# A new order of steps and of PSUM places in a one-core kernel of shift-mix, state space, attention and two mixture-of-experts stages

## The chip, the cores and the metric

The kernel runs on one core of a Trainium2 chip. The metric is the device time of one execution in microseconds. The engines are named as the profile names them: PE (TensorE, matrix products), PEld (its weight loads), ACT (ScalarE), DVE (VectorE), POOL (GpSimd) and SP (SyncE, which only issues transfers).

## What is computed

The input x has 1024 tokens of width 256, all in float32. Each stage adds its result to x. In shortened form:

```
x += shift_mix(norm(x))             # keys, values, receptance, a scan over time, an output product
x += first_ffn(norm(x))             # 8 experts, the best one of each token
x += state_space(norm(x))           # projection, convolution, scan in blocks, gated norm, output product
x += first_ffn(norm(x))             # the same weights again
x += attention_a(norm(x))           # 16 heads of 16 in 4 groups, causal
x += second_ffn(norm(x))            # 32 experts, the best 4 of each token, silu(gate) * up, down
x += attention_b(norm(x))           # 16 heads, 4 shared keys and values, a slope for distance
x += second_ffn(norm(x))            # the same weights again
```

An expert stage has to take to each expert the tokens that chose it, and to bring its rows back, weighted.

## The kernel before

**Groups and streams.** The tokens are cut into two groups of 512 (four tiles of 128). Each stage of each group is written as Python generators ("streams"); one call of a stream emits one step, a few instructions. A stream's name is a letter for the stage, the group, and a letter for the kind of step. The stages are A (shift-mix), F (first experts), S (state space), G (first experts again), a (attention a), e (second experts), b (attention b) and f (second experts again). So F1s is the sending of group 1's tokens to the first experts, and e0d the down products of group 0 in the second experts. Names without a group (k1, kf, la, lf, ls, l1, lw, cl, x0, x1, PS, P2) are loads, constants, clears and the switch between memory pools.

**The order is written out.** A string `ORDER` (L39 on) lists 2431 steps, and `follow` (L119) takes one step of the named stream for each entry. Every engine works its own instructions in the order in which they were emitted, and waits by semaphore for what it needs of others. A second string, `BANKS` (L105 on), gives each PSUM tile in turn one of eight places (`bank`, L142); a tile waits until the one before it in its place has been read.

**The expert stages.** In the second experts (`second_ffn`, L984) the steps are r (route: norm, logits, the four best, and ranks counted by matmuls at L1013 to L1018), s (16 sends by index on POOL, L1046, one for each tile and choice, which scatter rows of xn to a buffer in HBM sorted by expert), w (weights), f (16 fetches of a pair of experts by SP, L1073), t (turn: px transposes at L1082 on PE, copied to xT by ACT at L1086), g (gate: pgu products at L198, silu on ACT at L1098, a product on DVE at L1100), h (turn back: ph transposes at L1107, copied to hT by DVE at L1110), d (down: py products at L1118, copied to ye by DVE at L1122, stored by SP at L1124), b (16 fetches by index on POOL, L1134) and a (16 adds to x on DVE, L1144). xe has three buffers, xT, he, hT and ye two, yb six. The first experts (`first_ffn`, L374) do the same with eight experts: ranks at L415 to L419, four sends by index at L448, four fetches at L476, px at L483, xT at L488, py by L198, four fetches by index at L512, adds at L521.

```
for t in range(NT):
    for j in range(TOPK):
        nc.gpsimd.indirect_dma_start(
            out=sent_to[g][t * TOPK + j],
            out_offset=bass.IndirectOffsetOnAxis(ap=to[:, t, j:j + 1], axis=0),
            in_=xn[:, t, :], in_offset=None, bounds_check=ROWS - 1,
            oob_is_err=False)
        yield
```

**What lies beside what.** One group's experts are emitted between the steps of the other group's work. POOL has, beside the sends and fetches by index, the causal selects of the attention stages (L904), some row additions, small powers (L193) and a few constants. At the end the 16 fetches of f1b and their adds have nothing left beside them.

Of the kernel before, what the change touches and what calls it, by code (L numbers as in the profile page):

```python
# [36 lines left out]


ORDER = """  # L39
k1 A0n kf x0*2 kf A1n A0n*2 x0 A0n x0 A0n*3 la A0n*4 lf x1 A1n x1 A0n ka A0m0 x1 A1n*2 A0n*2 A0m0  # L40
x1 A1n*2 A0m0 la lf A0m0 A0k0 A0m2*2 A1n*3 A0m1 A1n A0m1*3 A1n*2 A1m0 A0k0*4 A0k1*5 A0k0*2 ls A0k0
la A0v0 A1m0 la lf*2 A1n lf A1n A1m0*2 A0m2 A0b A0v0*2 A0k1 kf A0v0*2 A0k1 A0m2 ls A0k1 A0m2 ls*2
A1k0*3 A0v1 A0r0*2 A0v1*2 A1k0 A0v1 lf A0v1 A0r1*2 A1m1 A1k1 la A0o A1k1*4 A0o*4 F0r*2 A0o*3 F0r*2
A1m1*2 F0r A1m1 A1v1 lf*2 F0r A1k1*2 A1m2 F0r*3 A1v0 A1v1*3 F0r*3 A1k1 A1v1 k1*2 ks kf*3 F0r*5 ls
k1 A1k0*2 A1m2*4 F0r*3 F0s*4 A1v0*2 F0f A1v0 A1k0*2 A1v0 A1r0*2 A1r1*2 A1b A1o*3 F1r A1o ks*3
A1o*3 F1r*2 F0f F0t A1o F1r*2 PS F0t*2 F0f*2 F0t*2 F1r*4 F0e F1r*3 lf F0e*2 F0t F0e*2 F1r*5 F0e*2
F0r F0t F1r*4 F1s F0e*2 F1s F0t F0e*3 F1s*2 F0w F0b F0a S0n F0b*2 F1f F0a F0b F0a S0n*2 F0a S0n
F1f S0n F1t*3 F1w F1e F1t F1f*2 F1t ks*2 S0n*8 F1e*3 F1t*3 S0d*2 F1e*3 S0d*5 S0u*2 S0c*3 S0h S0u
S0c*2 F1e*2 S0h*2 S0g*2 S0h F1e*2 S0h*5 S0c*5 F1e S0h*4 F1b S0g*5 F1a S1n F1b*3 S0g k1 F1a S0c*2
F1a S1n*2 F1a S1n*2 cl*2 S0h*4 S0d*2 S1n*3 k1 S0l*2 S1n S0m*4 k1 S0l*3 S0h*3 k1 S0h cl S0h*2 S1n*4  # L50
S0l cl S0l*3 S1g*2 S1c S1d*2 S1c*4 S0u*2 S0h S0v*2 S0l*2 S0v S1d S0v*3 S0l S0v S0l S1d S0u*2 S1d
S0o S0u S1h S0v*5 S0y S1h S0o*2 S0y*2 S0l*2 S0y S0z S0o S1c S1h S1g S0z*2 S1h S0z S1d S1h S1c
S1h*4 S0l S0z S1c S0o*3 S1h S0z*4 S1c*2 S0z S1h S0z*3 S0y S0z*4 l1*2 G0r S1d S0l*4 S1u*2 S0l S1c
S1h*6 S1c S0z*2 S0l G0r S0l S1u*2 S1h*3 cl S0l S0y*2 S1h*3 S0y S0z*2 S1h l1 S0z S0o S0z S1g*2 S1d
cl S1v S1d S1v*7 S1m*4 S1l*2 S0z*5 S1l*2 cl S0z*4 S1v*2 S0z*2 S1u*2 S0z*2 G0r S1v*2 S1l*3 S0z*2
G0r*2 S1l*5 S1o S1y*2 G0r S1u G0r S1u G0r*2 S1y*2 S1z G0r*4 k1 S1o*3 S1z*3 G0r S1g*3 G0r*4 S1z
G0r*2 G0w G0s*4 S1z G0f S1z*3 S1l G0f S1z*2 S1l*10 S1z*5 S1l S1z S1y*3 S1z*2 S1o*3 G0t S1y G0f
G0t*2 G0f l1 S1z*2 G0e*3 G0t*2 S1z G0t G0e*2 G0t*2 G0e S1o S1z*2 G0e*2 G1r*2 S1z G0e*4 S1z*10 l1
S1z*3 G0b G1r G0b G1r*2 G0b*2 G1r*6 G0a k1*3 G1r*3 G0a a0n*2 G0a a0n G0a a0n*9 G1r*3 a0n a0k a0q
G1r P2 a0q cl a0a cl*2 a0q*5 G1r*2 G1w a0k*5 a0p k1 G0r k1 a0p k1 G1s a0p cl*2 a0q a0p*7 a0v l1*2  # L60
a0b G1r a0b cl*3 a0p*2 a0v a0p G1s*3 G1f G1t*2 G1f G1t*2 a0p*3 G1f G1t G1f a0p*3 G1e*6 G1t*2 a0b
G1e*2 a0p G1e G1t G1e*2 a0p*4 a0w*6 a0b a0p*5 a0w*4 a0c a0p G1e G1b*3 G1a*2 a1n a0w G1b a0w*6
a0b*2 a0c a0f*3 G1a a1n*2 a0w*3 cl G1a lw*3 a0w*9 a0c a1n a0w a1n*2 a0w*3 a0p a0w*4 a0f a1n*4
a0p*2 a0f a1a a0p a0f*2 a1n*3 a0f e0r a0p*2 a0c a1k a0w*4 a0b a0f a0b a1k a0f a1q*4 a0w*4 a0c
a0w*4 a1q a1k a0f a1k*3 a0w*3 a1p*2 a0f*2 a1q a0f e0r a0f*3 l1*2 a1q*2 a0f*2 a1p*4 a0c a0f*5 a1p*2
a0f*3 a1p a0f e0r*3 a1b*2 a1p e0r*4 a1w*5 a1p*3 e0r a1p*2 e0r*9 a1w a1v*2 a1w*2 a1p*2 a1w e0r*3
a1w a1c a1f a1p*2 a1b*2 e0s a1p*5 e0s*4 a1p a1w*7 a1p*4 e0s*2 a1p*3 a1w*2 a1c lw*2 e0s*3 a1w*3 e0s
a1p*2 a1w*4 lw*4 a1b*2 a1w*3 a1f*2 a1w a1f*2 a1p*2 a1c a1w*3 a1c a1f lw e0s*3 e0w a1f*2 e0s*2 a1b
lw*2 e1r lw a1f*2 a1w*5 a1f a1b a1w*10 a1c a1f*5 e0f*2 e0t e0f*2 a1w*2 a1f a1w e0t a1w a1c a1f e0t
a1f*5 e0t a1f e0g a1f*2 e0g*4 a1f e0t*4 e0h e0g a1f e1r*4 e0h*3 e0g*4 e0f*2 e0t e1r*4 e0g e0d*2  # L70
e1r*4 e0d*2 e1r e0h e0d*2 e0g e0t e1r*2 e0g e0h*3 e0t*2 e1r*2 e0g e1r e0f*3 e0d*2 e0g*4 e0t*2 e0f
e0t e0d*2 e0t*2 e1r*2 e1s*5 e0h*3 e0g*4 e0t*2 e0f e0d*4 e1s e0g*2 e0f e0g e0t*3 e0f e1s e0f e0h*4
e0d*2 e0g e0d e1s*2 e0g*4 e0d*3 e0t*2 e0h e0g e0t*3 e0h*3 e0d*2 e0f*2 e0h e0g*3 e0d*3 e0g e1s*2
e0g e0d*5 e0h e0g e0h*2 e0t*4 e0g*2 e0d*2 e0g e0d e0h*3 e0d*2 e1s*4 e0d e1s e1f*2 e0g*4 e0h*2 e0d
e0g e0d e0t e0g*2 e1f e0h e0d*2 e0g e0h e0d e0h*2 e0d*3 e1t*3 e1f e0d*2 e1t e1g*2 e0d*2 e0b e1t*2
e1g*2 e1t e1h e1g*3 e1f e1h*2 e1f e1g e1h e1d*2 e1f e0b*2 e1d*2 e1g e1t e1g*3 e1t*2 e0b e1t*3
e1h*3 e1d e1g e1h e1f*3 e0a*4 b0n e1g*4 e1t e1d*2 e1t*2 e1d*3 e0b*2 e0a e1d*2 e0a e1h*2 e0b e0a
e1g*5 e1t*3 e1h e1g e1h e1f*3 e1g e0b*3 e1t e1d*5 e1h e1w e1h e0a b0n e1h e1g*3 e1t*2 e1d*2 e1h
e1g e1d e0b e1h e0b*2 e1t e1g e1d e1f e0a e1d e0b e1g*2 e0a*2 e1f e1t*2 e0b*2 e1d*2 e1h e1d e0a*5
e1t e1g*3 b0n*2 e1h*4 e1g*3 b0n e1g*2 b0n*4 e1d*2 e1t*2 e1d*2 b0a e1h*3 e1g e1t b0n*3 e1d*4 e1g*2  # L80
e1t e1d b0n b0q*2 e1g*3 e1d e1h*2 b0k*3 e1d*3 b0q*2 e1h b0k*2 b0q b0k b0p*2 b0q*3 e1f e1t b0p*3
e1t e1g*2 b0p e1g e1d e1h e1d e1h e1d b0b*2 e1h*2 b0p*3 b0w*4 e1d*5 b0p b0w*2 e1d b0p*4 b0w b0p*2
b0w b0p*2 b0w*2 b0v*2 b0b*2 e1d e1b e1a e1b*3 b0p*2 b0w b0p*4 e1a*2 e1b*2 b0w*2 b0c b0p*2 e1a e1b
e1a b0f*3 e1b e1a e1b b0p*4 e1b b0w*6 e1a b0c b0w*3 b0f b0p*3 b0w*4 e1a b0f*3 b0c b0f b0b*2 b0p*2
b0f*2 e1a*2 b0w*6 b0f*2 b0w*2 e1b*3 b1n b0c e1b*3 b0p b0b b0w*3 b0b e1a*3 b0w e1a b0w*6 e1a b0w*4
b0c e1a b0w*4 b1n*4 b0f*5 b1n*2 b0c b0f*3 b1n*3 b0f*4 b1n*3 b1k f0r b1k*3 b0f b1k b0f b1q*2 b0f
f0r b0f b1k b1q e1r b1q*2 b1p f0r*7 b1q*3 f0r*2 b1p f0r*2 b1p*2 f0r b1p*2 b1b f0r*2 b1b b1w*2
f0r*3 b1p*2 b1w*2 b1a b1p b1w*2 f0r*2 b1v*2 b1p*4 b1w b1p b1w*3 b1c b1p*4 b1f*2 b1p b1f b1b*2
b1p*3 f0s b1f b1p*3 b1f f0s*5 b1w*7 f0s*4 b1c b1w*7 b1p*5 b1f b1p*2 b1b*2 b1f b1w*2 b1c b1f b1p*2
f0s*4 b1p*2 b1w*7 b1b b1f f1r b1c f0s*2 f0f b1w*6 f0f b1w b1f b1b b1w b1f b1w*2 b1c b1w*2 b1f*6  # L90
b1w*3 f1r f0t b1w*4 b1f*2 b1c f0t b1f*4 f0g b1f*2 f0t f0f b1f*3 f1r*3 f0t f0g*5 f0f*2 f0t*4 f0h*3
f0g f0t f0g f1r f0f f1r*7 f0f*2 f0d f0g f1r f0h f0d*3 f0t*2 f1r*2 f0h f0d f0g*2 f0h f1r f0g f1r*2
f0g*3 f0t*3 f0d*3 f0h f0g f0t*2 f1r*2 f1s f0h*3 f0g*6 f0f f0t f0d*2 f0h f0d f1w f1s f0h f0f*3
f1s*2 f0d*2 f0h*2 f0d f0t*4 f0g f1s*4 f0g*4 f0d*2 f0f f0d*3 f0t*2 f0d f1s f0h*4 f0g f0f*2 f0g f0t
f0g*3 f1s f0g f0h f1s f0d*3 f0g f0d f0h f0t*2 f0d*2 f0f f1s*2 f0g*2 f0d*2 f0t f0d f0h f0d f0h*3
f0g*3 f0d*2 f0t*4 f0d*2 f0g*2 f1s*3 f1f*2 f0h*2 f0d*2 f0g*2 f0r f1f f0d f0g f0h*2 f0t f0g f0d f0g
f0d f0h*2 f0d f0g f1t*2 f0g f0h f1t*2 f1f*2 f0d*3 f1g*5 f1h f1t*2 f0d*2 f1t*2 f0h f0d f1g*2 f1h
f0d f1g*3 f1t f1h f1f*2 f0d f1d f1g f1t*3 f1f f1g*2 f1h*2 f1t f1d f1f f1g*3 f1d*2 f0w f1t f1h*4
f0b f1f f1t*3 f1d*3 f1g*3 f1h f1f f1t f1d*2 f1g f0b f1d f0a f1h*2 f1t f1d*2 f0a f1d f1g*2 f1d*3
f0b*3 f0a f1h f1f*2 f0a f0b f0a f1h f0b*2 f1g*5 f0b*2 f1d*5 f1h f1t f1g*3 f1t*4 f1h f0a f1h*2 f0b  # L100
f1h f0a f1f f1d*3 f0a f1g*2 f1t*2 f1d f1g*3 f1h f1f f0a*2 f0b f1d*3 z0*2 f1g*2 f1d*2 f1h*2 f1g*2
f1t*2 f1h*2 f1f f0b*3 f1d*6 f1t*2 f1g*3 f1h*2 f1g*2 f1h*2 f1d f1t f1r f1t f1g f1d f0a f1d*3 f1h
f1d f1h f1g f0b f1g*2 f1d f1h*2 f1d*5 f1b f0a*5 f1a f1b f1a f1b*3 f1a f1b*2 f1a*4 f1b f1a f1b*2
f1a f1b f1a*2 f1b f1a z0*2 z1*3 f1b*3 f1a*3 f1b f1a z1
"""  # L105


BANKS = """
012345670132465710324657132405713240537214063752140376215047632041763542076315247063201475147024
730247516204651247051624751602345160234602534602153460215346250734625073153416207543207413674213  # L110
056743025617432561743257641570321574032157430625741302657431027460253174602135674506724150367250
472502347165037146035274160532746105327465320714632140573106735406315047350647135076340753164075
364107534067134075163075146053714635071634056314075604751046351704635170463517043651074365107465
310740574603714603571430571430671430675140367514036275103462751034627103426710213416347106327016
203472013467210462731046237104237610427310642710346207416074601247602471620714607124627150246175
041627504162750412605174621504165720146570124657102465710432
"""

def follow(streams, order):  # L119
# [1509 lines left out]
```

## Time and profile before

| | us |
|---|---|
| runs | 785.84, 787.01, 790.27, 793.4, 797.79 |
| their median | 790.27 |
| the profiled execution | 786.36 |
| its span in the profile | 784.6 |
| DVE, ACT, POOL idle in the span | 295.4, 526.1, 498.0 |
| first and last matmul | 7.30, 752.3 |
| one send by index on POOL, and from one to the next | 0.98, 1.28 |
| one fetch by index, and from one to the next | 1.00, 1.31 |

The times in the profile are counted from the start of its span. In its rows an instruction stands with start, length, engine, line, operation, what it writes and reads, how many are taken together, and in brackets how long the engine had been idle before it and what ended that ("issue" and "remote" mean that the profile shows no such end, or one from outside the engine's own records). PEclk is the clock that PE was granted, as a share of the full one; in the page's row of slices it stands in tenths.

### The profile page before, as it was taken

The page shows a single profiled execution, that of the slowest core. Times are in us where ns is not written, and L with a number is a line of the kernel's source. Part 1 is how long each engine was busy: PE and PEld are TensorE (multiplying, and loading weights), DVE is VectorE, ACT ScalarE, POOL GpSimd, SP SyncE. Part 2 cuts the span into 40 slices and gives each one's busy share as a digit, 9 for nine tenths or more (in the row PEclk, how much of TensorE's full clock was granted, in tenths as well). Part 3 has the DMA queues.
Part 4 walks back from the last instruction along what each step waited for, and adds up shares of the span by engine and source line. Part 5 has one row for each costly group of instructions (what it writes and reads, how often), then busy time and mean ns, then how long its engine had stood idle before and what let it go on. Part 6 is the DMA issues. An engine that isn't in the chain of part 4 may idle for free. (4 is left out here: it accounts for less than half of the span.)

```text
span 784.6 us, 10048 instructions
## 1 busy us (share of the span) xinstructions
PE 642.4 (82%) x3168; PEld 432.7 (55%) x3168; DVE 489.2 (62%) x1507; ACT 258.5 (33%) x476; POOL 286.6 (37%) x333
## 2 busy tenths in 40 slices
PE   5657599999896999987994979999978999599930
PEld 2235464557584554443693968653443369498820
DVE  7987456998646676685371447577786537144642
ACT  4431134775521234322540222323520454122200
POOL 3124322443526234137216053136435421604435
PEclk9997889999896999998997998999997899899975
DMA  6602428000047238802245566212001124456833
GB/s 199 232 0 93 162 69 277 1 1 1 20 143 264 81 102 254 251 24 85 79 135 189 158 206 187 81 62 70 18 2 67 45 91 148 161 175 208 248 104 102
DMA packets 70827, 94.01 MB, mean 120 GB/s; under 512 B 6896, under 2 KB 60656, under 8 KB 70128
## 3 DMA queue, kind: packets, MB, share of 16 engines
q1 hardware_dynamic: 62944, 72.31, 28.7%
q0 software_dynamic: 7680, 20.98, 8.4%
q8 instruction: 27, 0.44, 0.3%
q14 instruction: 32, 0.26, 0.1%
q10 hardware_dynamic: 144, 0.01, 0.0%
HBM read 50.29 MB, written 42.99 MB: 119 GB/s over the span
## 5 line engine op out<-in xcount | busy, mean ns | idle before, releaser
L1134 POOL DMA_INDIRECT yb_f<-done,bk_f x64 | 65.2, 1019 | 110.8 <-issue 38.5
L198 PE MATMUL pgu_f<-gu,xT_f 128*128 128x192 f32 x512 | 98.0, 340 | 2.6 <-ACT xT_f L1086 2.5
L198 PEld LDWEIGHTS pgu_f<-gu,xT_f 128*128 128x128 f32 x512 | 88.9, 200 | 5.8 <-ACT xT_f L1086 3.9
L1046 POOL DMA_INDIRECT sent<-xn_f,to_f x64 | 62.9, 982 | 60.5 <-issue 19.4
L1118 PE MATMUL py_f<-dw,hT_f 96*128 96x256 f32 x256 | 67.5, 391 | 6.0 <-DVE hT_f L1110 5.4
L864 DVE CUSTOM_DVE_ANT_0 junk_b<-pS_b,tri 128x128 f32<-128x128 f32 (+1 forms) x128 | 45.7, 357 | 23.3 <-PE pS_b L851 15.5
L1122 DVE COPY ye_f<-py_f 128x512 f32<-128x512 f32 x64 | 43.8, 687 | 25.0 <-PE py_f L1118 9.1
L1098 ACT ACTIVATE he_f<-pgu_f 128x192 f32<-128x192 f32 x64 | 21.2, 332 | 106.5 <-PE pgu_f L198 55.9
L864 DVE CUSTOM_DVE_ANT_0 junk_a<-pS_a,tri 128x128 f32<-128x128 f32 (+1 forms) x128 | 45.7, 357 | 16.4 <-PE pS_a L851 6.6
L1118 PEld LDWEIGHTS py_f<-dw,hT_f 96*128 96x128 f32 x256 | 45.9, 195 | 13.2 <-ACT he_f L1098 4.4
L1100 DVE TENSOR_TENSOR he_f<-he_f,pgu_f 128x192 f32<-128x192 f32 x64 | 22.0, 349 | 47.9 <-ACT he_f L1098 29.5
L1086 ACT COPY xT_f<-px_f 128x512 f32<-128x512 f32 x64 | 36.6, 588 | 44.4 <-PE px_f L1082 25.0
L1110 DVE COPY hT_f<-ph_f 96x256 f32<-96x256 f32 x64 | 26.1, 414 | 30.0 <-PE ph_f L1107 19.0
L1144 DVE SCALAR_TENSOR_TENSOR x<-yb_f,wt_f,x 128x256 f32<-128x256 f32 x64 | 31.4, 496 | 19.0 <-DMA yb_f<-done,bk_f 18.5
L1107 PE MATMUL ph_f<-ident,he_f 128*96 128x128 f32 x128 | 24.5, 287 | 20.9 <-issue 8.9
L904 POOL TENSOR_SCALAR_AFFINE_SELECT pT_b<-pT_b 128x512 f32<-128x512 f32 x32 | 20.8, 670 | 56.4 <-ACT pT_b L901 56.2
L901 ACT ACTIVATE pT_a<-pST_a 128x512 f32<-128x512 f32 x48 | 25.6, 604 | 41.0 <-PE pST_a L893 26.5
L901 ACT ACTIVATE pT_b<-pST_b 128x512 f32<-128x512 f32 x48 | 26.2, 600 | 38.4 <-PE pST_b L893 29.6
L904 POOL TENSOR_SCALAR_AFFINE_SELECT pT_a<-pT_a 128x512 f32<-128x512 f32 x32 | 19.9, 645 | 50.4 <-ACT pT_a L901 50.4
L1082 PE MATMUL px_f<-ident,xe_f 128*128 128x128 f32 x256 | 36.7, 275 | 0.0
L893 PE MATMUL pST_b<-qm_b,kb_b 64*128 64x512 f32 x96 | 30.9, 692 | 2.9 <-ACT cT_b L946 1.5
L1082 PEld LDWEIGHTS px_f<-ident,xe_f 128*128 128x128 f32 x256 | 30.9, 142 | 3.1 <-issue 1.3
(298 smaller groups left out, 1335.1 us busy)
## 6 DMA issues: line engine op xcount, KB each, us to landing
xe_f<-sent SPq DMA_DIRECT2D x64, 256.0 KB
done<-ye_f SPq DMA_DIRECT2D x64, 256.0 KB
sent<-nil SPq DMA_DIRECT2D x16, 512.0 KB
xe_f<-fsent SPq DMA_DIRECT2D x16, 256.0 KB
fdone<-ye_f SPq DMA_DIRECT2D x16, 256.0 KB
gu<-in_L1f_gate SPq DMA_DIRECT2D x4, 768.0 KB
gu<-in_L1f_up SPq DMA_DIRECT2D x4, 768.0 KB
dw<-in_L1f_down SPq DMA_DIRECT2D x4, 768.0 KB
```

The source lines that it names most:

```text
L198: nc.tensor.matmul(dst, w(c), rhs(c), start=(c == 0), stop=(c == n - 1))
L864: nc.vector.tensor_tensor_reduce(out=junk[:, :w], in0=both[r][:, at:at + w], in1=tri[:, S - w:], scale=1.0, scalar=NEG, op0=ALU.add, op1=A ...
L893: nc.tensor.matmul(pS, kb[rows, s, k0:k0 + P], qm[rows].rearrange("p c q -> p (c q)"), start=True, stop=True)
L901: nc.scalar.activation(pT.rearrange("p c q -> p (c q)"), pS, AF.Exp)
L904: nc.gpsimd.affine_select(pT, pT, pattern=[[0, AG], [1, P]], compare_op=ALU.is_ge, fill=zero, base=0, channel_multiplier=-1)
L1046: nc.gpsimd.indirect_dma_start(out=sent_to[g][t * TOPK + j], out_offset=bass.IndirectOffsetOnAxis(ap=to[:, t, j:j + 1], axis=0), in_=xn[:, ...
L1082: nc.tensor.transpose(px[:, j * P:(j + 1) * P], xe[q][:, k, c * P:(c + 1) * P], ident)
L1086: nc.scalar.copy(xT[q].rearrange("p k c t -> p (k c t)"), px)
L1118: nc.tensor.matmul(py[:, k * D:(k + 1) * D], hT[q][:, k, :], dw[:, 2 * q + k, :], start=True, stop=True)
L1122: nc.vector.tensor_copy(ye.rearrange("p k d -> p (k d)"), py)
L1134: nc.gpsimd.indirect_dma_start(out=yb, out_offset=None, in_=done[g], in_offset=bass.IndirectOffsetOnAxis(ap=kept_["back"][:, t, j:j + 1], ...
L1144: nc.vector.scalar_tensor_tensor(x[g][:, t, :], due[t, j], kept_["wt"][:, t, j:j + 1], x[g][:, t, :], ALU.mult, ALU.add)
```

## The change

The change rewrites the two strings and nothing else. `ORDER` holds the same 2431 steps in another sequence, and `BANKS` other places for the PSUM tiles. No computation, buffer, transfer or constant is added or left out. Seen engine by engine:

- POOL has e0s as 7 sends, four selects of the attention and 9 sends (7, 3, 1 and 5 with selects between, before); e1s and f1s as 16 in a row, as before; f0s as 9, four selects and 7 (10 and 6 before); e1b as 9, four selects and 7 (10 and 6 before). The last two fetches of f0b stand behind the last down step of f1, just ahead of f1b. Between F1s and F0b stand a memset and four one-column selects. F1b lies in shorter pieces among the steps of S0.
- On PE the ranks of F1 stand behind two of F0's four py (three before), and px 2 and 3 of F0 behind them. e1s starts with 21 of e0's 32 t steps, 25 of 48 g, 11 of 32 h and 14 of 48 d emitted (17, 18, 8 and 10 before); f1s with 22, 25, 13 and 12 of f0's (16, 16, 7 and 8 before).
- At the start, more of POOL's constants are made before the first norm's power, four small DVE operations on the constants of A stand between the two halves of the first norm, and x's fourth tile is loaded behind wg. Three clears stand ahead of the loads of the first experts' weights.
- ACT loads a function table 31 times (29 before).

A core of the diff, the parts around F1's and e1's sends:

```diff
-A1o*3 F1r*2 F0f F0t A1o F1r*2 PS F0t*2 F0f*2 F0t*2 F1r*4 F0e F1r*3 lf F0e*2 F0t F0e*2 F1r*5 F0e*2
-F0r F0t F1r*4 F1s F0e*2 F1s F0t F0e*3 F1s*2 F0w F0b F0a S0n F0b*2 F1f F0a F0b F0a S0n*2 F0a S0n
...
-e0t e0d*2 e0t*2 e1r*2 e1s*5 e0h*3 e0g*4 e0t*2 e0f e0d*4 e1s e0g*2 e0f e0g e0t*3 e0f e1s e0f e0h*4
-e0d*2 e0g e0d e1s*2 e0g*4 e0d*3 e0t*2 e0h e0g e0t*3 e0h*3 e0d*2 e0f*2 e0h e0g*3 e0d*3 e0g e1s*2
```

In the new list the same stretches read, with other line breaks:

```
A1o*3 F0t*3 F0e F1r*12 F0e*2 F0t F0e F1r*4 F0f F1r*2 F1s*2 F0t*4 F0e F1w F0e*3 F1s*2 k1*2 F0w F0e*4
F0b F0a F1f F1t F1f S0n F0b*3
...
e1r e0g*2 e1r e1s e0h*2 e1s*3 e0t e1s e0h e0d e0g*3 e0d*4 e0h*3 e0g e1s*2 e0h e1s*2 e0d e0t*3 e1s*2
e0g*2 e0f e0g*2 e1s*2 e0d*3
```

## The prediction

> **What bounds the kernel now.** I read the page first, then what TensorE (PE) waited for, then a table by stretches, then single rows of the timeline.
>
> ```profile
> PE 642.4 (82%) x3168; PEld 432.7 (55%) x3168; DVE 489.2 (62%) x1507; ACT 258.5 (33%) x476; POOL 286.6 (37%) x333
> ```
>
> PE is busy 642.4 of 784.6 us, so 142.2 us are idle. 32.3 of these are the tail behind the last matmul (752.3 to 784.6); 109.9 lie between matmuls. The second view names the longest of those, by what ended each.
>
> ```profile
> PE px_f L483 <- DMA xe_f<-fsent: 9.0, 1, 9.0
> PE ph_f L1107 <- issue: 8.9, 2, 5.7
> PE ph_f L1107 <- ACT xT_f L1086: 7.8, 1, 7.8
> PE pST_a L893 <- DVE qm_a L878: 6.9, 3, 5.7
> ...
> PE py_f L1118 <- DVE hT_f L1110: 5.4, 4, 4.0
> ```
>
> Only the first is a plain wait for data: F1's tokens have to be sent by index and fetched. The others fall into long series of sends by index on POOL, as the table by stretches shows.
>
> ```profile
> core 0: us, PE busy (x) PEld busy (x) DVE busy (x) ACT busy (x) POOL busy (x), PEclk, DMA share, GB/s
> 347.00:366.00 19.00, 12.39 (x64) 6.23 (x64) 11.81 (x57) 4.13 (x8) 13.88 (x16) 0.93 0.21 76
> ...
> 408.00:431.00 23.00, 12.12 (x75) 10.91 (x74) 5.45 (x14) 3.46 (x8) 15.67 (x16) 0.79 0.55 183
> ...
> 664.00:687.00 23.00, 13.30 (x71) 11.93 (x70) 6.19 (x14) 3.58 (x9) 14.65 (x15) 0.85 0.53 171
> 752.00:784.60 32.60, 0.31 (x2) 0.00 (x0) 10.69 (x22) 0.00 (x0) 16.01 (x16) 0.56 0.37 107
> ```
>
> The first three are the sends e0s, e1s and f1s. No engine is full there. What is late shows in f1s, on PE and ACT:
>
> ```profile
> 668.60 2.77 PE L198 MATMUL pgu_f<-gu,xT_f 128*128 128x192 f32 x16
> 677.08 0.66 PE L1107 MATMUL ph_f<-ident,he_f 128*96 128x128 f32 x2 [5.72 <-issue]
> ```
>
> ```profile
> 676.31 0.33 ACT L1098 ACTIVATE he_f<-pgu_f 128x192 f32<-128x192 f32 x1 [9.31 <-remote]
> ```
>
> The pgu products end at 671.37, and ACT, with nothing else to do, starts on them at 676.31: it learns of PE's end 5 us late, and PE stands dry. That happens only some time into an unbroken series. The series of before and PE's idle time in or right behind each: 4 sends (5 us) none; 7 fetches at 523.90 (8.9 us) 1.4; 10 sends at 591.65 (12.6) 2.8; 10 fetches at 456.02 (13.0) 5.7; 15 sends at 664.06 (18.9) 9.7; 16 sends at 408.56 (20.2) 10.9. So PE loses about the series' length less 9 us. This is a fit to six rows, an estimate.
>
> **The change part by part.** The two lists hold the same 2431 steps; only order and PSUM places differ, so PE's, DVE's and DMA's work stays and what changes is who waits. Sum against the profiled execution's 786.36 us; the median of the runs shown, 790.27, is 3.91 above it.
>
> *F1's wait, -3.2.* Before, px 0-3 and py 0-2 of F0 stand ahead of F1's rank matmuls (L415) and one py behind; after, px 0-1 and py 0-1 ahead, so two px (0.60 each, row at 85.62) and one py (1.97, row at 83.81) lie beside the sends instead: 3.2 of 9.0. Between F1's sends and F0's fetches POOL now does a one-column memset and four selects (0.10, as neghalf's at 0.93, and 4 x 0.25, the row at 241.96: 1.1 us), which delay F0's adds and with them the state stage; F1's own four px and four py, some 10 us (4 x 0.60 + 4 x 1.97), cover it mostly: +0.5 (0 to +1.1). F1's wait can't go away: after 5.2 us of cover its fetch is still the last to come.
>
> *e0s, -4.4.* Before, POOL does 7 sends, a select, 3 sends, a select, 1, two selects, 5. After: 7, four selects, 9. Before loses the wait of 5.72 us, and PE's clock stays halved behind it:
>
> ```profile
> 364.00:367.00 3.00, 2.63 (x7) 1.12 (x8) 0.32 (x1) 1.07 (x4) 2.39 (x4) 0.50 0.00 0
> 367.00:370.00 3.00, 3.00 (x9) 0.88 (x7) 2.26 (x13) 0.56 (x2) 2.39 (x3) 0.50 0.39 134
> 370.00:375.00 5.00, 5.00 (x32) 2.34 (x32) 1.74 (x12) 2.93 (x6) 2.55 (x4) 0.98 0.27 81
> ```
>
> Six us at half rate cost 3.0. If series of 9.0 and 11.2 us follow the fit, 0 and 2.2 are left and 6.5 won; if the nine stop PE as before's ten did, nothing. Bounds 0 and -8.7 (all of it gone). The rows differ for ten in a row (2.8 and 5.7), so I take the middle, -4.4. What comes late next is e0's first fetch, behind the last send; steps of attention a (w and f) are listed between, so PE has work.
>
> *f0s and e1b, -0.6.* Both lists make runs of 9 and 7, parted by four selects, of before's 10 and 6. For f0s 2.8 becomes 2.2 by the fit (bounds -2.8 and +2.9, the other ten's 5.7). e1b was already spread by its adds (7, 3, 4, 2): 0.
>
> *e1s and f1s, 0.* In POOL's list of after these are still 16 sends in a row, with nothing between. Bounds: -10.3 (half of 10.9 + 9.7) and +10 (5 us each, below). They start later against the other group's experts: at the first e1s the list leaves some 24.6 us of PE's work (30 before), at the first f1s 24.7 (31.8). Needed are 15 x 1.28 = 19.2 us to the last send and 5.8 from there to px, as in F1 (92.13 to 97.94): 25.0. Work left and PE's lost time together cover that.
>
> *Tail, +0.5.* It keeps 16 fetches of 1.31 us each behind the last store. Two fetches of f0b now stand just ahead of them: 2 x 1.31 = 2.6, but POOL waits 4.36 us there (753.04 to 757.40), which holds them if their stores are done. Bounds 0 and +2.6.
>
> *Start, +0.5.* Four small DVE operations (omt to negw, 8.68 to 9.15: 0.47 us) come between the halves of the first norm, and a load (0.43, SP) ahead of x's fourth tile; bounds 0 and +0.9. POOL's memsets fit ahead of rstd_a at 5.74, in 4.08 us of its idle time. SP's three clears of 512 KB go ahead of F0's loads, which are needed from 62 us on: 0, but later if SP were full.
>
> *ACT's table loads, +1.3.* 31 for 29; two of 1.28 us each. ACT is 33% busy, yet its loads stand in PE's chain at times: half of 2.6; bounds 0 and +2.6.
>
> *PSUM places, 0.* A tile that waits for its place would show as a short wait of PE. All waits under 0.8 us make up 13.0 (109.9 less 96.9 in longer ones); a quarter of that either way, -3 to +3, bounds it, and no row tells a side.
>
> Sum: -3.2 + 0.5 - 4.4 - 0.6 + 0 + 0.5 + 0.5 + 1.3 + 0 = -5.4, so 781.0 profiled and 784.9 as a median.
>
> A rule that speaks against the change: sends laid beside other engines' work might be slowed by it. Rows first: the period is 1.28 us in 347 to 357, with DVE busy 8.32 of 10 us, and 1.28 in 408 to 420, with DVE busy 4.08 of 12. The Trainium skill (SBUF — State Buffer, "Who interferes with whom") says that a DVE operation in a two-port mode shuts GpSimd out for its whole length, and that software-generated DMAs suffer by it. If each of e0s' nine waited for one 0.69 us DVE copy, e0s would end 6.2 us later and the sum come to +0.8; by the rows it is nothing, and I go by the rows.
>
> **The rivals.**
> 1. *Nothing won but F1.* The change doesn't shorten what hurts: the two 16s remain, and nine in a row is nearly ten. For it: POOL's list. Against it: four selects in one place give PE's messages a gap. e0s and f0s at 0: 784.9 + 4.4 + 0.6 = 789.9.
> 2. *Slower: the late messages find PE with less unlocked work.* Place: the first us of e1s and f1s. ACT starves already 3 to 5 us into a series (413.34 and 667.00) and PE runs on until 418.51 and 671.36, on what was turned and gated before. With fewer turns and gates listed around the sends in after (during f1s 5 turns and 10 gates, against 15 and 25), PE may run dry 5 us sooner in each, and e0s' nine as before: 784.9 + 10 + 4.4 = 799.3. It decides once more than some 13 us of that happen (784.9 to 798.2).
> 3. *Faster by more.* With turns and gates out of the way, the handoffs that hurt are fewer: half of e1s' and f1s' loss gone, 784.9 - 10.3 = 774.6. For it: DVE and ACT idle 5 to 9 us at a time there, only because PE's word is late. Against it: the down steps need the same word.
>
> **How the numbers follow.** Likeliest 0.38 (own range 779 to 789), rival 1 0.18, rival 2 0.26, rival 3 0.18. A measurement tells about 1% from no change: below 782.4 or above 798.2. Faster: rival 3's 0.18 and a third of the likeliest, 0.31. Slower: most of rival 2, 0.24. Same: 0.45. The range takes in rivals 2 and 3 with some 2 us around: 772 to 802. Below it would be a gain at e1s and f1s beyond half, above it one more uncovered wait.
>
> **What would show it.** F1's px wait at about 5.8 us in place of 9.0. PE's wait in e0s at 0 to 3 us, and no half clock behind it. PE idle some 10 us in each of e1s and f1s, at a period of 1.28. A tail of 32 to 33 us. The first matmul 0.5 us later. The prediction is wrong if a wait over 3 us stands at a new place, if px of e1 or f1 waits for its fetch, or if e1s or f1s loses below 5 or over 14 us.

## The result and the profile after

The change made the kernel slower by 0.65%: the ratio is 1.0065, with a 95% interval of 1.0044 to 1.0086. The median of 38 runs was 798.75 us, that of 75 runs of before 791.63; the ratio, like every one below, is of the runs within 1.5% of the fastest of their kernel, and these two medians of all runs lie 0.9% apart. The forecast was 784.9, a gain of 0.7%.

Other engines learn that PE has ended a product by an update of PE's semaphore, its message. Before, after and the kernels below were run in several sets. In some sets none of PE's messages was late and the kernel before took 739 us; in others they were late, as in the profile of before, and it took 784 to 792. It never changed within a set. I call this "on time" and "late". The result above is of late runs, and every ratio below compares kernels of one set.

The profiled execution of after took 793.99 us, its span is 792.2, 7.6 more than before's. The page's line of busy times, then PE's longest waits:

```profile
PE 654.4 (83%) x3168; PEld 434.0 (55%) x3168; DVE 490.0 (62%) x1507; ACT 260.4 (33%) x478; POOL 285.5 (36%) x333
```

```profile
PE ph_f L1107 <- remote: 10.5, 1, 10.5
PE pt_a L248 <- DVE xn_a L239: 9.4, 3, 7.8
...
PE ph_f L1107 <- DVE he_f L1100: 6.4, 5, 4.7
PE py_f L1118 <- DVE hT_f L1110: 6.1, 2, 5.6
PE px_f L483 <- DMA xe_f<-fsent: 5.9, 1, 5.9
```

F1's wait has gone from 9.0 to 5.9, and e0s' wait of 5.7 is no longer in the list; the waits in e1s and f1s (ph_f, py_f) are as long as before. PE is busy 12 us longer for the same 3168 products. So the loss is not in the few long waits but in PE's own time. The next table parts PE's time from its first product to its last. Half of the busy time at clock 0.5 is counted as lost, which is an estimate (four px take 0.60 to 0.63 us at full clock and 1.08 at half). The stage of e0s is taken between the 1166th and the 1376th product: by then all these kernels have done the same number of products of each kind, but for two at most.

| us | idle | lost at half clock | busy, less that |
|---|---|---|---|
| whole, late: before, before_2 | 102.6, 94.3 | 38.7, 39.4 | 603.7, 604.2 |
| whole, late: after, after_2 | 97.7, 88.9 | 41.2, 34.6 | 613.2, 613.0 |
| whole, on time: paced_f1 (below), after_3 | 65.6, 71.6 | 28.0, 48.9 | 601.0, 609.2 |
| stage of e0s, late: before, before_2 | 9.9, 7.8 | 2.9, 5.7 | 37.2, 37.0 |
| stage of e0s, late: after, after_2 | 9.0, 8.3 | 1.7, 1.7 | 42.6, 42.6 |
| stage of e0s, on time: paced_f1, after_3 | 6.5, 5.5 | 0.0, 0.0 | 37.5, 42.6 |

Late, waiting and half clock fell by 6.3 us (mean of the two pairs), and PE's products themselves took 9.5 and 8.8 us longer, and 8.2 on time. More than half of that lies in the stage of e0s, 5.5 us. The products that grew most are pctx, the weighted sums of the attention: before's two lines, then after's.

```profile
L915 PE MATMUL pctx_b<-pT_b,vaug 128*32 128x512 f32 x96 | 16.2, 608 | 0.4 <-ACT pT_b L901 0.4
L915 PE MATMUL pctx_a<-pT_a,vaug 128*32 128x512 f32 x96 | 15.6, 606 | 0.0
...
L915 PE MATMUL pctx_b<-pT_b,vaug 128*32 128x512 f32 x96 | 21.3, 614 | 4.1 <-ACT pT_b L901 3.0 <-DVE vaug L832 0.6 <-POOL pT_b L904 0.5
L915 PE MATMUL pctx_a<-pT_a,vaug 128*32 128x512 f32 x96 | 16.5, 627 | 5.4 <-ACT cT_a L946 3.0 <-POOL pT_a L904 2.4
```

The eight products of a pctx take 1.06 us when all that they read is ready (first row, before). In after PE comes to them while POOL's causal selects are still to be done, gets two of them through, waits, and needs 1.63 for the other six:

```profile
344.85 1.06 PE L915 MATMUL pctx_a<-pT_a,vaug 128*32 128x512 f32 x8
...
348.43 1.05 PE L915 MATMUL pctx_a<-pT_a,vaug 128*32 128x512 f32 x2
350.12 1.63 PE L915 MATMUL pctx_a<-pT_a,vaug 128*32 128x512 f32 x6 [0.65 <-POOL pT_a L904]
```

In the stage of e0s the 40 products of pctx take 5.1 us in before and before_2 and 8.3 in after and after_2, full clock counted. The table by stretches answers to before's (from about the first send of e0s, e1s and f1s, and the tail):

```profile
355.00:374.00 19.00, 15.12 (x70) 6.84 (x66) 12.94 (x68) 4.51 (x10) 11.34 (x13) 0.91 0.16 56
420.00:443.00 23.00, 11.57 (x65) 9.92 (x64) 6.79 (x20) 2.42 (x7) 15.64 (x16) 0.82 0.44 152
680.00:703.00 23.00, 13.38 (x66) 11.16 (x66) 5.92 (x15) 2.65 (x6) 14.76 (x15) 0.73 0.48 167
759.60:792.20 32.60, 0.27 (x2) 0.00 (x0) 12.20 (x28) 0.00 (x0) 17.31 (x17) 0.54 0.39 116
```

In e1s PE does 65 products in 23 us where before did 75, in f1s 66 for 71. What is late is the same as before, and once worse: the silu for which PE's product has long been there.

```profile
427.50 1.47 PE L198 MATMUL pgu_f<-gu,xT_f 128*128 128x192 f32 x8
429.89 1.13 PE L1118 MATMUL py_f<-dw,hT_f 96*128 96x256 f32 x4 [0.92 <-issue]
441.53 0.66 PE L1107 MATMUL ph_f<-ident,he_f 128*96 128x128 f32 x2 [10.51 <-remote]
```

```profile
440.76 0.33 ACT L1098 ACTIVATE he_f<-pgu_f 128x192 f32<-128x192 f32 x1 [13.96 <-remote]
```

The product ends at 428.97 and ACT starts at 440.76, 11.8 us later; the last of the 16 sends ends at 440.86.

Where the time went shows only when the kernels are compared at equal work. I gave each group of PE's products its usual time at full clock (the lower quartile over the traces), summed these along PE's order, and read off the clock at the same sums. The "before" on time is the kernel paced_f1 below, which is before but for three one-column copies by POOL within f1s (0.2 us each; on time none of them waited). Where two numbers stand, they are two executions each (before, before_2; after, after_2).

| stretch of PE's work, us | before, late | after, late | before, on time | after, on time |
|---|---|---|---|---|
| 0 to 240 (all up to e0's routing) | 334.1, 331.8 | 337.1, 331.4 | 336.0 | 342.5 |
| 240 to 270 (attention a, e0s) | 45.7, 46.1 | 50.6, 49.8 | 39.6 | 45.4 |
| 270 to 330 (e0's experts, e1s) | 75.9, 73.3 | 76.1, 74.1 | 62.1 | 70.2 |
| 330 to 390 (e1's experts, e0b) | 75.4, 73.4 | 75.2, 74.4 | 67.1 | 68.7 |
| 390 to 420 (attention b, e1b) | 36.1, 36.0 | 42.3, 39.1 | 35.0 | 38.3 |
| 420 to 450 (attention b, f0s) | 50.3, 49.4 | 46.2, 45.1 | 45.0 | 44.8 |
| 450 to 510 (f0's experts, f1s) | 79.1, 79.8 | 78.9, 76.3 | 63.8 | 62.5 |
| 510 to the end of PE (f1's experts) | 55.3, 55.0 | 53.2, 53.3 | 53.1 | 64.5 |

Late, the new order loses 4.3 us at e0s and 4.7 at e1b, wins 4.2 at f0s and 1.9 in each of the last two, and the rest is within the scatter: about 2 us more in all from 240 on. These entries hang on the prices: with other ways to price a product e0s' loss comes out between 0.6 and 5.8 us. Between points of equal products, as in the table above, it is 3.3 and 2.1 us (53.4 for 50.1, 52.6 for 50.5), and e1b and f0s together, from the 1940th product to the 2604th, lose 1.2 in one pair and win 2.5 in the other. So the loss at e1b and the gain at f0s, which are neighbours, mostly cancel. On time the new order loses 28.7 us from 240 on. The on-time columns are single executions, and the one of after (771.1 us) was 6.5 above the median of its four.

### The profile page after: what moved, and what is told of

Same layout as the page of the kernel before. It is cut to its first block, busy times and chain, and to the rows that moved or that the text cites. A ratio compares the mean times of both kernels' runs of the same rounds, so it can differ in the third digit from the quotient of the medians.

```text
span 792.2 us, 10065 instructions
## 1 busy us (share of the span) xinstructions
PE 654.4 (83%) x3168; PEld 434.0 (55%) x3168; DVE 490.0 (62%) x1507; ACT 260.4 (33%) x478; POOL 285.5 (36%) x333
## 4 chain that ended last, share of the span: by engine, by line
PE 54%; DVE 11%; issue 6%; POOL 4%; DMA 4%; another core or an unknown queue 3%; ACT 3%; POOLq 0%; DVEq 0%; ACTq 0%
PE pgu_f L198 9%; PE py_f L1118 6%; PE pST_b L893 4%; PE px_f L1082 3%; PE pS_b L851 3%; PE pST_a L893 2%; PE pctx_b L915 2%; PE pS_a L851 2%; PE py_f L198 2%; PE pq_a L198 2%; PE ph_f L1107 2%; PE pq_b L198 2%; DVE junk_a L864 1%; DVE x L1144 1%
## 5 line engine op out<-in xcount | busy, mean ns | idle before, releaser
L198 PE MATMUL pgu_f<-gu,xT_f 128*128 128x192 f32 x512 | 95.8, 332 | 0.5 <-ACT xT_f L1086 0.2
L198 PEld LDWEIGHTS pgu_f<-gu,xT_f 128*128 128x128 f32 x512 | 85.2, 194 | 2.6 <-ACT xT_f L1086 0.7
L1046 POOL DMA_INDIRECT sent<-xn_f,to_f x64 | 62.9, 982 | 59.5 <-issue 19.9
L1118 PE MATMUL py_f<-dw,hT_f 96*128 96x256 f32 x256 | 69.9, 404 | 7.8 <-DVE hT_f L1110 6.1
L864 DVE CUSTOM_DVE_ANT_0 junk_b<-pS_b,tri 128x128 f32<-128x128 f32 (+1 forms) x128 | 45.7, 357 | 23.8 <-PE pS_b L851 13.9
L1118 PEld LDWEIGHTS py_f<-dw,hT_f 96*128 96x128 f32 x256 | 47.8, 202 | 16.1 <-issue 9.2
L864 DVE CUSTOM_DVE_ANT_0 junk_a<-pS_a,tri 128x128 f32<-128x128 f32 (+1 forms) x128 | 45.7, 357 | 15.2 <-PE pS_a L851 8.3
L1098 ACT ACTIVATE he_f<-pgu_f 128x192 f32<-128x192 f32 x64 | 21.1, 332 | 90.9 <-PE pgu_f L198 50.5
L1144 DVE SCALAR_TENSOR_TENSOR x<-yb_f,wt_f,x 128x256 f32<-128x256 f32 x64 | 31.6, 501 | 15.8 <-DMA yb_f<-done,bk_f 12.0
L904 POOL TENSOR_SCALAR_AFFINE_SELECT pT_a<-pT_a 128x512 f32<-128x512 f32 x32 | 20.1, 652 | 52.0 <-ACT pT_a L901 51.9
```

The costliest lines, as they stand in the source:

```text
L198: nc.tensor.matmul(dst, w(c), rhs(c), start=(c == 0), stop=(c == n - 1))
L864: nc.vector.tensor_tensor_reduce(out=junk[:, :w], in0=both[r][:, at:at + w], in1=tri[:, S - w:], scale=1.0, scalar=NEG, op0=ALU.add, op1=A ...
L904: nc.gpsimd.affine_select(pT, pT, pattern=[[0, AG], [1, P]], compare_op=ALU.is_ge, fill=zero, base=0, channel_multiplier=-1)
L1046: nc.gpsimd.indirect_dma_start(out=sent_to[g][t * TOPK + j], out_offset=bass.IndirectOffsetOnAxis(ap=to[:, t, j:j + 1], axis=0), in_=xn[:, ...
L1118: nc.tensor.matmul(py[:, k * D:(k + 1) * D], hT[q][:, k, :], dw[:, 2 * q + k, :], start=True, stop=True)
```

## The experiments

The kernels of the first kind are made of the two lists: up to some step one order, then what is left in the other, each step with its PSUM places of the list that it comes from.

**Which part costs.** early_after takes the new order up to e0's third routing step, late_after from there on, e0s_after only from there to e1's fifth routing step.

```
early_after: new[... e0r, e0r] + rest in the old order
late_after:  old[... e0r, e0r] + rest in the new order
e0s_after:   old[... e0r, e0r] + new[... e1r*4] + rest in the old order
```

> The new order up to the third routing step of e0 (about 340 us), then what is left in the old order. Theory (the loss is made in the stage of e0's sends, 337 to 394 us, where after takes 57 us and before 49): as before within 2 us, since both traces had done the same work at 337 us. Rival (the loss comes in many places, by the new PSUM places or the late parts alike): 2 to 4 us slower than before.

> The old order up to the third routing step of e0, then what is left in the new one. Theory (loss in the stage of e0's sends): 5 to 8 us slower than before, all that the whole change costs. Rival (many places): 2 to 4 us slower.

> The old order, but from the third routing step of e0 to the fifth of e1 (about 340 to 400 us) the new one. Theory (loss in this stage): 5 to 8 us slower than before. Rival (the loss comes later, at e1b and f0s, where the traces drift apart by 3 us more): within 2 us of before.

All three ran on time (before 739.17): early_after 749.91, ratio 1.0161 (1.0118 to 1.0204); late_after 758.35, 1.0263 (1.0223 to 1.0304); e0s_after 747.18, 1.0122 (1.0086 to 1.0158). e0s_after lost 9 us (6 to 12 by its interval) where the theory had 5 to 8. But early_after, from which nothing was expected, lost 12, and late_after 19. The theory of one stage fell.

The three losses are not prices of three parts, for a seam puts steps side by side that neither list has there. Set against paced_f1 at equal numbers of products, early_after is 2.6 us behind just ahead of its seam (product 1166, 335 us) and 8.7 behind at product 1248, with PE's clock at 0.52 from 343 to 357; e0s_after loses 8.3 us between products 1376 and 1524, at its second seam. PE's busy time, less what half clock cost, is 601.0 us in early_after, the same as in paced_f1. In e0s_after it is 605.3, with 42.7 for 37.5 in the stage of e0s: this stage's order is what makes PE busy 5.2 us longer there.

**Half of the sends.** half_sends leaves out the third and fourth choices of group 1, from the kernel before.

```diff
                 for j in range(TOPK):
+                    if g == 1 and j > 1:
+                        yield
+                        continue
```

> The kernel before, with only the first two of four choices of group 1 sent in both second expert stages, so e1s and f1s have 8 sends each instead of 16 (the third and fourth choices of group 1 are left out of the experts' input; all the rest is done). Theory (PE's messages come late once a series is longer than some 9 us, so PE loses the length less 9): series of 10.0 us, PE's idle time in them 1 us each instead of 10.9 and 9.7, and 16 to 24 us off the whole with the half clock behind. Rival (PE stands for other reasons there, memory traffic or buffers): PE still idles 7 us or more in each, and at most 6 us off the whole.

On time: 737.25 against 739.17, 0.998 (0.9949 to 1.0011). Neither side of that expectation could show, for no message was late. The same kernel where messages were late:

> The kernel before with two of four choices sent for group 1 (the third and fourth are left out of the experts' input). Where no message is late it was the same as before (0.998). Theory (late messages grow with the length of a series): if messages are late here, 14 to 24 us faster than before; if not, the same again. Rival (late messages come with something else, the experts' stage or its memory traffic): within 6 us of before in both cases.

768.30 against 785.19, 0.9811 (0.9749 to 0.9873), 15 us off: the theory. The rows of e1s and f1s of half_2, in the columns used above, have PE busy 20.5 and 20.8 of 23 us, against 12.1 and 13.3 with 16 sends (before):

```profile
407.00:430.00 23.00, 20.53 (x128) 18.94 (x127) 10.22 (x23) 5.55 (x14) 7.77 (x8) 1.00 0.59 194
647.00:670.00 23.00, 20.76 (x129) 18.68 (x128) 11.53 (x31) 5.53 (x14) 7.85 (x8) 1.00 0.63 201
```

**Before and after again.** Both lists unchanged.

> The changed kernel once more. In the four runs so far no message of PE came late and before took 739 us instead of 790. Theory (what the change wins is less waiting for PE's late messages, and apart from that its order is the worse one): where messages come late, 0 to 1% slower than before; where none does, 2.5 to 4.5% slower (1.6% and 2.6% were measured for its two halves alone). Rival (the change costs the same everywhere): 0.7% slower in both cases.

> The kernel before once more, for its profile. Theory: 785 to 797 us with some 10 us of PE's idle time in each of e1s and f1s if PE's messages come late in it, 735 to 745 with less than 2 us in each if not; nothing between.

> The changed kernel again, for its time where PE's messages are on time. Theory (the new order costs 4% by itself and wins 3% by less lateness): 3 to 5% slower than before if no message is late, within 1% of before if they are. Rival (the halves' costs do not add up, since a group that is late in one half has time in the other): 1 to 2.5% slower if no message is late.

after_2 ran late: 784.82 against 785.19, 0.9988 (0.9949 to 1.0027), no slower, where the theory had 0 to 1%. before_2, in the same set, took 779.15 us, lower than expected by 6. after_3 ran on time: 764.66 against 739.21, 1.030 (1.0217 to 1.0384), the theory: the new order costs 22 to 25 us by itself where no message is late, and nothing to 0.65% where they are. Some 8 us of it are PE's longer products (609.2 for 601.0). Another part shows in PE's waits of after_3:

```profile
PE px_f L1082 <- DMA xe_f<-sent: 11.4, 3, 8.0
```

```profile
445.81 0.63 PE L1082 MATMUL px_f<-ident,xe_f 128*128 128x128 f32 x4 [2.78 <-DMA xe_f<-sent]
...
683.20 1.08 PE L1082 MATMUL px_f<-ident,xe_f 128*128 128x128 f32 x4 [7.99 <-DMA xe_f<-sent]
```

These are the first px of e1 and of f1: they wait for the fetch behind the sixteenth send, since too little of the other group's work is left to lie beside the series. The same two waits stand in the other on-time profiles with the new order there: 2.5 and 7.3 us in late_after, 2.7 and 8.0 in after_e0s_old, 3.1 and 7.9 in e0s_spread. With before's order px waits 0.5 us at most on its fetch (early_after, e0s_after, paced_f1). The stage behind the second one (510 to the end) takes 64.5 us for 53.1.

**Are these waits the cost?** after_half takes the same half of the sends from the changed kernel.

> The changed kernel with only the first two of four choices of group 1 sent (the third and fourth are left out of the experts' input), so e1s and f1s end 10 us sooner. Theory (the new order leaves too little work beside these sends, and px waits for them): where messages are on time, the waits of 2.8 and 8.0 us go and with their half clock 10 to 16 us come off, 1.0 to 1.7% slower than before instead of 3.0%; where they are late, 14 to 24 us off, as from the kernel before. Rival (the cost of the new order lies elsewhere): where messages are on time, 2.5 to 3.5% slower than before still.

It ran late: 772.64 against 783.88, 0.9838 (0.980 to 0.9875). After was not run in this set; by its ratio in the other late sets (1.0065 and 0.9988) that is 18 or 12 us off, at one end inside the 14 to 24 of the late half of the expectation and at the other below it. The question is left: that the two waits are a part of what the order costs on time is read from the traces and was not tested. The new order with f1's routing as early as in the old one was not tried.

**What in e0s costs.** after_e0s_old undoes the order of e0s' stage in after; e0s_spread moves nine sends.

```
after_e0s_old: new[... e0r, e0r] + old[... e1r*4] + rest in the new order
e0s_spread:    e0s*7 select e0s*2 select e0s*2 select e0s*2 select e0s*3   (after: e0s*7 select*4 e0s*9)
```

> The changed kernel with the old order in one stage only, from the third routing step of e0 to the fifth of e1. By equal work of PE this stage took 50.9 and 50.2 us in after, 45.5 and 45.9 before, where PE's messages come late. Theory (the new e0s stage costs 5 us by itself): the stage back at 44 to 47 us and 3 to 6 us off after, so at or below before. Rival (what is saved there comes back as waiting later, since the two groups only change places): the stage shorter, the whole within 1.5 us of after.

> The changed kernel with the nine last sends of e0s moved between the four causal selects ahead of them (2, 2, 2 and 3 behind one each), nothing else. Theory (POOL waits for ACT between these selects and then holds the next selects up for 11 us): e0s ends 4 to 7 us sooner, the stage takes 45 to 48 us instead of 50, 2 to 5 us off after. Rival (the stage is long because PE's messages are late or because routing starts later, whatever the sends' place): stage at 49 to 51 us, no gain.

Both ran on time, at 739.58 for before: after_e0s_old 766.53, 1.0389 (1.0311 to 1.0466); e0s_spread 764.70, 1.0328 (1.0267 to 1.0388). Neither is below after's 1.030. With the old order of the stage, after_e0s_old has PE's products there back at 37.7 us (42.6 in after_3); by the table's stretches the stage took 43.5 us for 45.4. Nothing of it came through to the end: behind its first seam PE's clock is 0.5 for 13.7 us from 340.8, at a cost of 6.8 us of PE's time. In e0s_spread the stage took 51.1 us. Its series lasted 22.4 us, where after's on time (after_3) lasts 23.6 and 27.5 late, so on time there was little to win. And it delayed selects that pctx waits for: the 40 products of pctx take 9.9 us instead of 8.3. The selects that stand behind the nine sends, as here in after (late),

```profile
382.02 0.97 POOL L1046 DMA_INDIRECT sent<-xn_f,to_f  x1 [0.30 <-issue]
383.00 1.23 POOL L904 TENSOR_SCALAR_AFFINE_SELECT pT_a<-pT_a 128x512 f32<-128x512 f32 x2
```

are thus not what makes that stage long on time. Neither kernel was run late. What is shown is that the stage's order makes PE's products some 5 us longer (it comes with the new order in e0s_after and goes with the old in after_e0s_old, and 3.1 us of it are pctx). That the broken pctx are the reason is read from the rows, and what a mend of them alone would win was not tried.

**Cutting the series.** paced, paced2 and paced_f1 start from the kernel before. Ahead of every fourth send POOL copies one column that DVE has just set to zero, so it waits until DVE is there in the list.

```diff
+                if <series> and t > 0:
+                    nc.vector.memset(tok, 0.0)
+                    nc.gpsimd.tensor_copy(got, tok)
                 for j in range(TOPK):
```

paced cuts e1s and f1s at the old places of the list, paced2 all four series with the groups moved apart, paced_f1 and paced_f1_2 (the same kernel, run again) f1s alone at the old places.

> The kernel before, but POOL waits ahead of every fourth send of e1s and f1s for a small memset that DVE does where the list has that send, so the 16 sends come as four series of 5 us. Theory (only unbroken series make PE's messages late): if messages are late here, PE's idle time in e1s and f1s falls from some 10 us to 0 to 4 us each and the time by 8 to 18 us; if not, it costs 0 to 6 us, since sends end later. Rival (the number of sends matters, not the break): no gain in either case.

> The kernel before with all four series e0s, e1s, f0s and f1s cut into fours: the groups of four sends stand some 7 us of work apart in the list, and ahead of each POOL waits for a small memset on DVE. Theory (PE's messages are late only some 5 to 9 us into an unbroken series): if they are late here at all, PE idles under 3 us in each of the four and 10 to 20 us come off before; if not, within 4 us of before. Rival (it is the number of sends, or the experts' traffic, broken or not): PE still idles 8 us or more in e1s and f1s together and the time is within 5 us of before.

> The kernel before, with POOL waiting ahead of every fourth send of f1s alone for a small memset of DVE, at the old places of the list. Theory (the loss is the series' length less 9 us, and f1s has slack behind it): where messages are late, PE's idle time in f1s falls from 10 us to 2 to 5 us and 4 to 9 us come off before; where not, within 3 us of before. Rival (what is saved comes back as waiting for the fetch behind the later sends): within 2 us of before or slower.

> The kernel before, with POOL waiting ahead of every fourth send of f1s for a small memset of DVE. Where messages are late, 4 to 9 us off before if the loss is the series' length less 9 us; within 2 us of before if the later sends take it back. Where they are on time: within 3 us of before.

paced, late: 782.46 against 785.19, 0.9979 (0.9949 to 1.0009), no gain that can be told. DVE ran ahead, so e1s came as 12 in a row and 4, not as four fours, and e1's px then waited 4.66 us for its fetch; f1s came as 11 and 4 behind its first (3.5 us of waiting ahead of the four). The expected 8 to 18 us did not come. paced2 ran on time: 759.33 against 739.58, 1.0284 (1.0236 to 1.0332), 20 us slower where 4 were allowed; the groups end later, and px of e1 and f1 waits 7.1 us in all and pctx 6.4 (in paced_f1 0.4 and none). It was not run late. paced_f1, on time: 738.29 against 739.21, 0.9982 (0.9942 to 1.0023). paced_f1_2, late: 776.50 against 783.88, 0.9873 (0.9811 to 0.9936). So this kernel is 1.3% faster than before where messages are late (four runs) and no slower that can be told where they are not. POOL waited once in its f1s, 3.5 us behind the twelfth send. Its row of f1s (659 to 687) beside e1s, which it leaves alone:

```profile
408.00:431.00 23.00, 14.17 (x81) 12.87 (x80) 5.49 (x14) 3.46 (x8) 15.63 (x16) 0.84 0.60 191
659.00:687.00 28.00, 23.85 (x136) 21.40 (x135) 11.40 (x34) 6.11 (x15) 15.22 (x18) 0.94 0.65 206
```

**Writes or making.** no_write sends all of group 1 to indices out of bounds, so POOL makes the sends and nothing is written.

```diff
+            if g == 1:
+                nc.vector.memset(far, 1e6)
+                nc.vector.tensor_copy(to, far)
```

> The kernel before, with every index of e1s and f1s out of bounds, so that the 32 sends of group 1 are made by POOL and write nothing (group 1's tokens reach no second expert). If the writes hold PE's messages up, PE's idle time in e1s and f1s falls under 3 us each and the time by 14 us or more, if messages are late here at all; if making the sends on POOL does it, all stays as before within 5 us.

> The kernel before, with every index of e1s and f1s out of bounds: POOL makes the 32 sends of group 1 and they write nothing (group 1's tokens reach no second expert). If the writes hold PE's messages up, PE's idle time in e1s and f1s falls under 3 us each and the time by 14 us or more, where messages are late; if making the sends on POOL does it, within 5 us of before. Where no message is late: within 5 us of before.

> The kernel before, with every index of e1s and f1s out of bounds: POOL makes the 32 sends of group 1 and they write nothing (group 1's tokens reach no second expert). Where messages are late: 14 us or more off if the writes hold PE's messages up, within 5 us of before if the making on POOL does. Where they are on time: within 3 us of before.

On time: 738.62 in a single run, and 738.65 against 739.21, 0.9989 (0.9957 to 1.0022). Late: 786.77 against 783.88, 1.0031 (0.9999 to 1.0064). The DMA's traffic in e1s falls from 183 to 93 GB/s, and PE stands nearly as it did (busy 12.6 and 15.3 us for 12.1 and 13.3):

```profile
411.00:434.00 23.00, 12.63 (x74) 11.33 (x73) 5.10 (x13) 3.02 (x8) 15.62 (x16) 0.78 0.31 93
665.00:688.00 23.00, 15.27 (x81) 13.46 (x80) 7.08 (x18) 3.50 (x9) 14.60 (x15) 0.90 0.35 102
```

So it is not the rows written that go with the late messages. It is the making of the sends on POOL or the handling of their packets, which are still queued: in 20 us of e1s the queue of the sends (q0) has as many as before, almost empty (first line before, 408 to 428; second no_write_3, 411 to 431).

```profile
q0 software_dynamic: 672, 1.84, 25.1%
...
q0 software_dynamic: 720, 0.01, 2.3%
```

These two were not told apart.

## Why the prediction was wrong

The range, 30 us wide, held the time; the sign was wrong.

**The step that failed** stands ahead of the terms: "PE's, DVE's and DMA's work stays and what changes is who waits." PE's own time was so put at nothing, for the reason that the steps are the same. Measured, PE's busy time at full clock rose by 9.2 us for the same products (603.7 and 604.2 to 613.2 and 613.0; on time 601.0 to 609.2). 5.5 us of it lie in the stage of e0s, where the prediction had its largest gain. A product of pctx that comes before its inputs are ready breaks its group of eight, and the group then takes longer. The gain in waiting that was forecast did come: idle time and half clock fell by 2.4 and 10.2 us in the two pairs, 6.3 in the mean, against 8.2 in the terms of F1, e0s and f0s. (The prediction's 109.9 us between matmuls have the 7.3 ahead of the first one with them, and its list left out the longest entry, pt_a with 11.7, which has these 7.3 in it.) The terms, in their order:

- **F1's wait, -3.2: right by itself, and given back.** The wait fell from 9.0 to 5.9. But F0's fetches by index started at 97.29 instead of 93.47, 3.8 us later, where the prediction had +0.5 for a memset and four selects. F1's sends began 1.0 later, the memset and selects took 1.1, as forecast, and the largest part, 2.06, is in POOL's row: it waits for the store of the py that was moved behind the sends:

```profile
94.29 0.94 POOL L1449 TENSOR_SCALAR_AFFINE_SELECT slope<-slope 128x1 f32<-128x1 f32 x4
97.29 1.06 POOL L512 DMA_INDIRECT yb_f<-fdone,bk_f  x1 [2.06 <-DMA fdone<-ye_f]
```

  The prediction counted the moved px and py as cover for the sends and did not follow them to their store, which the next fetches need. PE reached the same work (60 us of it) at 114.0 and 114.3 us before, 115.7 and 112.5 after.
- **e0s, -4.4: here the step failed.** The wait of 5.72 did shrink, to one of 3.00 us (at 363.08), and the half clock from 2.9 and 5.7 us lost to 1.7. But at equal products the stage took 3.3 and 2.1 us more (4.3 by the prices), since PE's products took 42.6 instead of 37.1. The first send came 8.0 and 3.5 us later than before and the last ended 11.4 and 6.4 later. The prediction reckoned with the series' lengths alone and took the stage's other steps as they were; these had all been moved.
- **f0s and e1b, -0.6.** By the prices the stretch of f0s won 4.2 and that of e1b lost 4.7. Together, at equal products, they came to +1.2 and -2.5, so the sum of the term is not refuted; its parts are not what was forecast. After has nine fetches in a row at e1b, but PE waits nowhere over 2.2 us there; pctx is again what takes longer (19.9 and 20.1 us for 15.4 and 15.8 in the two stretches).
- **e1s and f1s, 0: right as to PE's idle time.** 11.4 us (0.92 + 10.51) for 10.9, and 9.6 (4.03 + 5.59) for 9.7. The clause "Work left and PE's lost time together cover that" is right for late messages alone: on time, with 24.6 and 24.7 us of work for the 25.0 needed, px waits 2.8 and 8.0 us, the second far more than the sum's 0.3. That clause hid that the kernel's time hangs on lateness.
- **Start, +0.5; tail, +0.5.** The first matmul came 0.46 later in the first pair (7.76 for 7.30) and 0.08 in the second (7.39 for 7.31): within its bounds, and not told from scatter. PE's end to the span's end is 32.3 us in both: the two late fetches cost nothing. The table loads (31 for 29) could not be told from the rest.
- **Period of the sends.** It is 1.28 us in after too (371.79 to 373.08 and on), with DVE busy 4.21 of 13 us around the nine and 6.79 of 23 in e1s. The rule of the Trainium skill that the prediction weighed (SBUF — State Buffer, "Who interferes with whom") has no visible part in this result.
- **The fit, length less 9 us.** It holds roughly for the series that were cut: 8 sends (10.0 us) left PE 2.5 us of idle time in 23 against a forecast of 1; f1s as 11 (13.9 us) and 4 left 4.0 (paced) and 4.2 (paced_f1_2) in 28, against 4.9 forecast and 9.7 uncut. But it described the late runs only; nothing in one profile told that there are others.
- **Rival 2** named the right sign and the wrong mechanism: in e1s PE ran dry 8.3 us after the first send (10.0 before), in f1s 7.2 us after the 15 sends began (7.3 before), not 5 us sooner.

What remains: late, less waiting against longer products, seen in two pairs of executions. Of the 9.2 us some 6 are pctx (31.8 to 37.8 by the lines above); the rest of the longer products was not traced to its reason, and no kernel with whole pctx in the new order was run.

## What to carry to other kernels

When a step is moved to cover one transfer, follow it to everything that waits for its own result: a store that comes later delayed the next fetch by index here by 2.1 us, of 3.2 that the cover was to save. The same products can take an engine longer in another order: 9.2 us here, which no list of waits shows, so compare busy time at equal products as well as waits. When the whole order is new, the long waits of the old profile are a small part of the story; compare at equal work of the bounding engine, stretch by stretch, before believing any one wait. A tuned order may be fitted to a disturbance: time it with the disturbance and without, and prefer an edit that, like the cut of f1s alone, gains in one and costs nothing that can be told in the other.

## What the runs showed of the hardware

In the sets where PE's messages were late, the recorded updates of PE's semaphore came up to 7.1 us (before) and 12.6 us (after) after PE's instruction had ended, all of them (but for the last us of the kernel) in series of sends or fetches by index on POOL or at most 3 us behind; in before no update of ACT, DVE or POOL in the body of the kernel was over 0.6 us late, in after one of DVE (1.1). In the other sets none of PE's was over 0.6 us late (again but for the last us), with the same series at the same period, and PE was busy without a break through both e1s and f1s (paced_f1, on time; in early_after, whose f1s has no copies in it, also 23.00 of 23 from 637 to 660):

```profile
404.00:427.00 23.00, 23.00 (x144) 21.38 (x143) 12.38 (x28) 6.97 (x17) 15.63 (x16) 1.00 0.77 254
626.00:649.00 23.00, 23.00 (x147) 21.66 (x146) 12.90 (x38) 5.89 (x14) 16.29 (x19) 1.00 0.78 252
```

Together this is 45 to 52 us of the kernel before (783.88 to 791.63 against 739.2). Sets of both kinds bore the same chip number, so it is not shown to belong to a chip; what sets it off was not found. PE's clock was 0.5 for 3.4 to 17.1 us at a time behind PE's longer waits in both kinds of sets. Eight products of pctx took 1.0 us when none of them waited, and 2.7 us of PE's busy time when a wait of 0.65 us came between the second and the third.
